# Norms of q and k with tokens on partitions in a convolution-attention kernel

## The chip, the cores and the metric

The kernel runs on one core of one Trainium2 chip. The time is the device time of one execution in microseconds (us); the time of a kernel is the median of several runs. A core has five engines that work side by side and meet through semaphores: PE (TensorE, matrix products from SBUF into PSUM), DVE (VectorE), ACT (ScalarE), POOL (GpSimd) and SP (which here only starts transfers). Each runs its own instructions in order. POOL and SP start the transfers (DMA). PEld is the loading of the stationary operand of a product; it is listed apart from PE.

## What is computed

The network has two layers: a convolution attention on a 64 x 64 image of 256 channels, then a bidirectional state-space block and a mixture of experts on the 4096 tokens. The change touches the first layer alone:

```python
qkv = concat([conv(x, W1, 0), conv(x, W3, 1), conv(x, W5, 2)], axis=1)
qkv = conv(qkv, Wdw, 1, groups=3 * c)          # 3x3, each channel by itself
q, k, v = split(qkv, 3, axis=1)                # 8 heads of 32 channels
n = sqrt(sum(t * t, axis=-1, keepdims=True))   # over the 32 channels of a head
t = t / maximum(n, 1e-12)                      # for t = q and t = k
attn = softmax(einsum('bhnc,bhmc->bhnm', q, k) * temperature)
```

So each token needs, for q and for k, eight norms, one per head, and each of its 256 values is divided by the norm of its head. q is also multiplied by the temperature of its head.

## The kernel before

All values are fp32. `conv_phase` (from L174) keeps channels on partitions: 256 channels are two halves t = 0, 1 of 128 partitions, so a half holds four heads. Tokens run along the free dimension, in eight chunks of N = 512.

**Order.** Everything from L605 on stands in a manual schedule: each engine runs its instructions in the order in which the program issues them. The work is cut into twelve units (kind, half of the image, t): four units of k, then q and v in turn, four of each. A unit of k or v makes 6 or 8 products by Winograd's method (L452, 6 or 10 matrix products of 512 columns in each), a unit of q makes 4 plain ones (L444). `feed` issues products ahead, up to three results (four PSUM buffers, pool `a_pcv`). `transform_out` combines the results on DVE (`out_t`, `pad`; ACT copies every second result out of PSUM first, tile `c`, L481), in groups of two. `depthwise` of a unit runs during the unit after it: ACT starts it with the first tap of two pieces (L524), DVE adds the other eight taps of each (L528, 16 instructions). In each group of a unit the program issues, in this order: the combination, `feed`, `tick`, the steps of `depthwise`, and "fills" (transforms of the weights, `wx` and `wo`, and of the inputs, `v`).

**Norms.** When `depthwise` of a unit of q or k has ended, its finished rows wait in `rows_left` as chunks of 128 channels x 512 tokens: three for the upper part of the image, five for the lower. `norm_sums` takes up to three chunks at a time, and the next three only once these are done. It has three steps, each one `tick` after the one before it:

- `norm_sums`: ACT squares each chunk (`sq`, L550) and PE multiplies the squares by `heads` (L551). `heads` is the stationary operand, 128 x 32, and the 512 columns of `sq` move. Each chunk's result has 32 partitions of its own in one PSUM tile (`ps`, tag ps0): eight copies of each head's sum.
- `norm_inverse`: over up to 96 partitions x 512 tokens, DVE takes the maximum with 1e-24 (L558), ACT the square root (L559), DVE the reciprocal (L560). PE spreads the four rows of each chunk over its 128 channels by a product with `pick`, or `pick_q`, which holds the temperature (L565; 32 partitions, 512 columns).
- `norm_apply`: DVE multiplies the chunk by the result in PSUM (L275, `acc<-acc,ps`). For q, ACT puts the columns into another order (`qo`, L574). POOL starts the store (L578).

The program has twelve such rounds, here called g1 to g12. The column "DVE next" is the first instruction on DVE behind L560.

| round | chunks | squares on PE (L551) | maximum (L558) | spread on PE (L565) | DVE next |
|---|---|---|---|---|---|
| g1 | 3 | 151.72 | 166.93 | 171.80 | 171.57 |
| g2 | 3 | 225.23 | 239.73 | 244.60 | 244.37 |
| g3 | 3 | 301.82 | 312.82 | 337.39 | 317.47 |
| g4 | 3 | 355.82 | 356.99 | 374.18 | 361.64 |
| g5 | 3 | 385.74 | 386.90 | 391.78 | 391.56 |
| g6 | 3 | 420.51 | 427.69 | 442.60 | 432.33 |
| g7 | 1 | 461.03 | 472.71 | 477.48 | 477.35 |
| g8 | 3 | 497.79 | 504.20 | 527.46 | 508.85 |
| g9 | 2 | 549.63 | 550.75 | 567.97 | 555.40 |
| g10 | 3 | 582.96 | 584.13 | 611.62 | 591.51 |
| g11 | 3 | 666.64 | 694.13 | 703.14 | 705.25 |
| g12 | 2 | 709.41 | 711.87 | 716.75 | 718.82 |

(us from the start of the span, in the profile of before.) `heads`, `pick` and `pick_q` are made on DVE and PE at the very start (L227 to L260), among the statistics of the input (L611), outside the manual schedule.

**Buffers.** `sq`, `c`, `wx`, `wo`, `qo` and the copies of v share one pool of six buffers (`a_t`, tag "t"). `heads`, `pick` and `pick_q` lie in the pool `a_one` with the large tiles; `rn` lies in `a_r`. The pools close at the end of `conv_phase`. Then `Early` loads weights of the second layer (`win`, `wx`, `wdt`, L746 to L752) and `attention_phase` loads `wpj`, q and k (L832 to L850), all on SP's queue, in this order.

Of the kernel before, what the change touches and what calls it, by code (L numbers as in the profile page):

```python
# [14 lines left out]
FP = mybir.dt.float32  # L15
# [3 lines left out]
AF = mybir.ActivationFunctionType  # L19
ALU = mybir.AluOpType  # L20
AX = mybir.AxisListType
# [3 lines left out]
P = 128  # L25
# [3 lines left out]
CT = C // P  # L29
N = 512  # L30
# [143 lines left out]
def conv_phase(cx, xT, w1, w3, w5, temp, qd, kd, vd, uk, uv):  # L174
# [13 lines left out]
    nc, tc = cx.nc, cx.tc  # L188
# [3 lines left out]
    with ExitStack() as ctx:  # L192
        one = ctx.enter_context(tc.tile_pool(name="a_one", bufs=1))
        up = ctx.enter_context(tc.tile_pool(name="a_u", bufs=3))
        rp = ctx.enter_context(tc.tile_pool(name="a_r", bufs=1))
        tp = ctx.enter_context(tc.tile_pool(name="a_t", bufs=6))
        accp = ctx.enter_context(tc.tile_pool(name="a_acc", bufs=3))
        pcv = ctx.enter_context(tc.tile_pool(name="a_pcv", bufs=4, space=PSUM))
        pms = ctx.enter_context(tc.tile_pool(name="a_pms", bufs=1, space=PSUM))
# [24 lines left out]
        for t in range(CT):  # L224
            nc.sync.dma_start(out=wq[:, t, :], in_=w1[t, 0, :, 0, :])

        heads = one.tile([P, 32], FP, name="heads")  # L227
        pick = one.tile([P, P], FP, name="pick")
        nc.vector.tensor_reduce(
            pick.rearrange("p (a b) -> p a b", b=32)[:, :, 0:1], cx.ident.rearrange("p (a b) -> p a b", b=32),  # L230
            AX.X, ALU.add,
        )
        nc.vector.tensor_copy(
            heads.rearrange("p (a b) -> p a b", b=8),
            pick.rearrange("p (a b) -> p a b", b=32)[:, :, 0:1].to_broadcast([P, 4, 8]),
        )
        first_of = one.tile([P, 32], FP, name="first_of")
        nc.vector.memset(first_of, 0.0)
        for h in range(4):
            nc.vector.memset(first_of[:, 8 * h : 8 * h + 1], 1.0)  # L240
        rep = one.tile([P, 4], FP, name="rep")
        for h in range(4):
            nc.vector.tensor_reduce(
                rep[:, h : h + 1], cx.ident.rearrange("p (j a) -> p a j", a=32)[:, 8 * h, :], AX.X, ALU.add
            )
        nc.vector.tensor_copy(pick.rearrange("p (a b) -> p a b", b=32), rep[:, :, None].to_broadcast([P, 4, 32]))

        pick_q = []
        for t in range(CT):
            x = tp.tile([P, 4, 32], FP, name="px", tag="t")  # L250
            nc.vector.tensor_scalar(
                x, heads[:, None, :].to_broadcast([P, 4, 32]), temp[:, t : t + 1], None, ALU.mult
            )
            y = one.tile([P, 4, 32], FP, name=f"px{t}")
            nc.vector.tensor_tensor(y, x, first_of[:, None, :].to_broadcast([P, 4, 32]), ALU.mult)
            ps = pms.tile([P, N], FP, name="ps", tag=f"ps{t}")
            nc.tensor.transpose(ps[:, 0:P], y.rearrange("p a b -> p (a b)"), cx.ident)
            pq = one.tile([P, P], FP, name=f"pick_q{t}")
            nc.vector.tensor_copy(pq, ps[:, 0:P])
            pick_q.append(pq)  # L260

        wdw = one.tile([P, 54], FP, name="wdw_s")
        for kind, f in ((0, 1.0), (1, -1.0 / 6.0), (2, -2.0 / 9.0)):
# [10 lines left out]
        def plus(out, x, y, op=ALU.add):  # L274
            nc.vector.tensor_tensor(out, x, y, op)  # L275
# [231 lines left out]
        def depthwise(kind, half, t, pad):  # L507

            row0, n = (LAG, H - LAG) if half else (0, LAG)
            ch = {"q": 0, "k": CT, "v": 2 * CT}[kind] + t  # L510
            dst = accp.tile([P, (H - LAG) * W], FP, name="acc", tag="acc")

            def piece(b, tap):
                dy, dx = divmod(tap, 3)
                m = n // 2
                return (
                    dst[:, m * W * b : m * W * (b + 1)].rearrange("p (h w) -> p h w", w=W),
                    pad[:, m * b + dy : m * b + dy + m, dx : dx + 4, :].rearrange("p h s j -> p h (s j)"),
                    wdw[:, 9 * ch + tap : 9 * ch + tap + 1],
                )  # L520

            for b in range(2):
                o, src, w_ap = piece(b, 0)
                nc.scalar.activation(o, src, AF.Copy, scale=w_ap)  # L524
            for b in range(2):
                for tap in range(1, 9):
                    o, src, w_ap = piece(b, tap)
                    nc.vector.scalar_tensor_tensor(o, src, w_ap, o, ALU.mult, ALU.add)  # L528
                    yield
                if kind == "v":  # L530
                    turn(dst, t, row0 * W // P, n * W // P // 2 * b, n * W // P // 2)
            if kind != "v":
                c0 = row0 // ROWS
                rows_left.extend((dst[:, N * j : N * j + N], kind, t, c0 + j) for j in range(n // ROWS))
                if not busy:
                    norm_sums()
# [3 lines left out]
        def norm_sums():  # L540

            chunks = rows_left[:3]
            del rows_left[:3]
            busy[:] = chunks
            if not chunks:
                return
            ps = pms.tile([P, N], FP, name="ps", tag="ps0")
            for j, (a, _, _, _) in enumerate(chunks):
                sq = tp.tile([P, N], FP, name="sq", tag="t")
                nc.scalar.activation(sq, a, AF.Square)  # L550
                nc.tensor.matmul(ps[32 * j : 32 * j + 32, :], heads, sq, start=True, stop=True)  # L551
            later(lambda: norm_inverse(chunks, ps))

        def norm_inverse(chunks, ps):

            n = 32 * len(chunks)
            rn = rp.tile([P, N], FP, name="rn", tag="rn")
            nc.vector.tensor_scalar(rn[0:n, :], ps[0:n, :], 1e-24, None, ALU.max)  # L558
            nc.scalar.activation(rn[0:n, :], rn[0:n, :], AF.Sqrt)  # L559
            nc.vector.reciprocal(rn[0:n, :], rn[0:n, :])  # L560
            back = []
            for j, (_, kind, t, _) in enumerate(chunks):
                back.append(pms.tile([P, N], FP, name="ps", tag=f"ps{j}"))
                r = slice(32 * j, 32 * j + 32)
                nc.tensor.matmul(back[j], (pick_q[t] if kind == "q" else pick)[r, :], rn[r, :], start=True, stop=True)  # L565
            later(lambda: norm_apply(chunks, back))

        def norm_apply(chunks, back):
            for (a, kind, t, c), ps in zip(chunks, back):
                plus(a, a, ps, ALU.mult)  # L570
                if kind == "q":

                    s = tp.tile([P, N], FP, name="qo", tag="t")
                    nc.scalar.copy(  # L574
                        s.rearrange("p (h j r) -> p h r j", j=TX, r=4), a.rearrange("p (h r j) -> p h r j", r=4, j=TX)
                    )
                    a = s
                nc.gpsimd.dma_start(out=(qd if kind == "q" else kd)[t][:, N * c : N * c + N], in_=a)  # L578
            norm_sums()

# [13 lines left out]
        def later(f, lag=1):  # L594
            events.append((clock[0] + lag, f))
# [9 lines left out]
        with tc.manual_schedule(engines=ORDERED):  # L605
# [13 lines left out]
            ps = pms.tile([P, N], FP, name="ps", tag="ps0")  # L619
# [7 lines left out]
            ps = pms.tile([P, N], FP, name="ps", tag="ps1")  # L627
# [1337 lines left out]
def kernel(  # L1965
# [45 lines left out]
    nc.vector.tensor_scalar(beyond, hottest, SAFE, None, ALU.is_gt)  # L2011

    conv_phase(cx, xT, w1, w3, w5, temp, qd, kd, vd, uk, uv)
    with tc.tile_pool(name="early", bufs=1) as pool:
        early = Early(cx, pool, w_in, w_x, w_dt)
# [105 lines left out]
```

## Time and profile before

| what | us |
|---|---|
| three runs | 4383.31, 4386.24, 4386.42; median 4386.24 |
| the profiled execution | 4368.56 |
| its span, first to last instruction | 4366.8 |
| busy over the span: PE, DVE, ACT, POOL | 3693.8, 3600.9, 2685.7, 1563.3 |
| first product of the attention (L953) | starts at 730.18 |
| squares on ACT, L550, 128x512 | 32 of 0.621 |
| squares times heads on PE, L551 | 64 records, 18.9 busy |
| maximum, L558, 96x512 | 9 of 0.681 (64x512: 2; 32x512: 1) |
| square root, L559, 96x512 | 9 of 0.629 |
| reciprocal, L560, 96x512 | 9 of 3.349 (64x512: 3.345; 32x512: 3.341) |
| spread on PE, L565 | 64 records, 19.5 busy |
| multiplication, L275 `acc<-acc,ps` | 32 of 0.681 |
| reordering of q, L574 | 16 of 1.125 |
| first tap on ACT, L524 | 0.922 (768 columns), 1.346 (1280 columns) |

One fp32 product shows as two records on PE and two on PEld. In the timeline each entry merges neighbours of one kind: its start, the time from the first start to the last end, engine, line, operation, out<-in, shapes, the number of instructions, and in brackets how long the engine had been idle and what ended that. The convolution phase fills about the first 722 us of the span; the attention and all that follows are not edited.

### The profile page before, as it was taken

To read this page: it belongs to the slowest core of one execution; us is meant where nothing else is said; L and a number is where in the kernel's file an instruction comes from. 1 tells how busy PE (TensorE), PEld (TensorE's weight loads), DVE (VectorE), ACT (ScalarE), POOL (GpSimd) and SP (SyncE) were. 2 spreads that over 40 slices of the span, in tenths; PEclk is the share of its full clock that TensorE was granted. 3 is DMA by queue.
4 is the path that set the end of the run, shared out by engine and by line. 5 is a ranking of instruction groups with operands and counts; after the bars stand their busy time and mean duration, and the time that the engine had idled before them with its cause. 6 is when DMAs were issued, how large, how long until landed. Compare 5 with 4: busy or idle time off the path is not lost. (4 is left out here: it accounts for less than half of the span.)

```text
span 4366.8 us, 43278 instructions
## 1 busy us (share of the span) xinstructions
PE 3693.8 (85%) x15072; PEld 1180.6 (27%) x15072; DVE 3600.9 (82%) x2976; ACT 2685.7 (62%) x4175; POOL 1563.3 (36%) x1051
## 2 busy tenths in 40 slices
PE   4659895999999999997878788888788788876698
PEld 2224341222222222222222222222222222221243
DVE  6887876888879879778899999999999999999311
ACT  1012223888788888776677777777777777774122
POOL 2210000000000000002677677776767777776000
PEclk9879996999999999998888989989888898977799
DMA  4322223000000000003332334443323334332121
GB/s 148 125 77 93 75 79 129 4 30 11 25 23 18 16 23 18 11 23 118 104 108 98 103 124 119 123 119 107 127 82 124 124 114 118 120 109 84 63 63 37
DMA packets 150243, 351.18 MB, mean 80 GB/s; under 512 B 35461, under 2 KB 44421, under 8 KB 149502
## 3 DMA queue, kind: packets, MB, share of 16 engines
q1 hardware_dynamic: 139214, 313.17, 23.1%
q0 software_dynamic: 10800, 35.14, 2.3%
q8 instruction: 120, 1.97, 0.2%
q14 instruction: 109, 0.89, 0.1%
HBM read 268.69 MB, written 79.56 MB: 80 GB/s over the span
## 5 line engine op out<-in xcount | busy, mean ns | idle before, releaser
L1669 POOL TENSOR_TENSOR dbx<-dtxr,b 128x1024 f32<-128x1024 f32 x512 | 1205.8, 2360 | 467.7 <-DVE da L1677 320.7
L1677 DVE TENSOR_TENSOR_SCAN da<-da,state,dbx 128x1024 f32<-128x1024 f32 x512 | 1203.2, 2350 | 62.0 <-ACT state L1700 33.6
L960 ACT ACTIVATE e<-sc 128x1024 f32<-128x1024 f32 x1024 | 992.8, 1023 | 204.7 <-PE sc L953 161.2
L881 DVE TENSOR_TENSOR s<-s,e 128x1024 f32<-128x1024 f32 x768 | 880.6, 1216 | 44.7 <-ACT e L960 44.2
L1659 ACT ACTIVATE da<-dtr,aneg 128x512 f32<-128x512 f32 x1024 | 708.3, 692 | 36.0 <-DMA dtr<-dtd 3.8
L953 PE MATMUL sc<-q,kS 32*128 32x512 f32 x4096 | 653.6, 644 | 20.4 <-DMA kS<-kd 11.4
L1682 DVE TENSOR_TENSOR h<-da,c 128x1024 f32<-128x1024 f32 x512 | 627.2, 1225 | 37.7
L888 PE MATMUL av<-e,vT 128*32 128x512 f32 x4096 | 549.8, 608 | 3.7 <-ACT o L894 3.7
L1709 PE MATMUL y<-h,sel 128*32 128x512 f32 x2048 | 442.0, 675 | 130.9 <-DVE h L1682 130.7
L132 POOL TENSOR_TENSOR ln_few<-ln_few,minus_half 128x4 f32<-128x4 f32 x29 | 29.4, 1015 | 1417.8 <-DMA ln_few<-ln_row 1417.8
L452 PE MATMUL cv<-v,u 128*128 128x512 f32 x928 | 422.2, 615 | 64.4 <-DVE pad L272 27.4
L953 PEld LDWEIGHTS sc<-q,kS 32*128 32x128 f32 x4096 | 211.3, 183 | 466.9 <-issue 244.4
L1250 PE MATMUL mm<-u,win 128*128 128x512 f32 x496 | 267.2, 688 | 72.0 <-DMA u<-ud 52.4
L1700 ACT COPY state<-da 128x2 f32<-128x2 f32 x511 | 80.5, 158 | 362.5 <-DVE h L1682 360.0
L452 PEld LDWEIGHTS cv<-v,u 128*128 128x128 f32 x928 | 182.1, 198 | 302.9 <-issue 230.9
L528 DVE SCALAR_TENSOR_TENSOR acc<-pad,wdw_s,acc 128x768 f32<-128x768 f32 (+1 forms) x192 | 244.5, 1279 | 19.4 <-ACT acc L524 13.3
L1294 PE MATMUL mm<-xp,taps 128*128 128x512 f32 x480 | 221.3, 609 | 6.0 <-DVE m L1441 5.1
L881 DVE TENSOR_TENSOR s<-e 128x1024 f32<-128x1024 f32 x128 | 150.8, 1219 | 71.6 <-ACT e L960 71.4
L888 PEld LDWEIGHTS av<-e,vT 128*32 128x32 f32 x4096 | 81.3, 108 | 396.6 <-issue 379.0
L1709 PEld LDWEIGHTS y<-h,sel 128*32 128x32 f32 x2048 | 60.4, 114 | 468.5 <-DVE h L1682 292.8
L1250 PEld LDWEIGHTS mm<-u,win 128*128 128x128 f32 x496 | 104.2, 221 | 244.8 <-issue 127.0
L504 ACT COPY pad<-pad 128x480 f32<-128x480 f32 x12 | 7.1, 594 | 214.2 <-DVE pad L272 214.1
(338 smaller groups left out, 3747.3 us busy)
## 6 DMA issues: line engine op xcount, KB each, us to landing
dtr<-dtd SPq DMA_DIRECT2D x128, 512.0 KB
dtxr<-dtd SPq DMA_DIRECT2D x128, 512.0 KB
b<-bcd SPq DMA_DIRECT2D x64, 256.0 KB
c<-bcd SPq DMA_DIRECT2D x64, 256.0 KB
dtd<-dt SPq DMA_DIRECT2D x64, 256.0 KB
dtd<-few SPq DMA_DIRECT2D x64, 256.0 KB
u<-uv SPq DMA_DIRECT2D x24, 640.0 KB
u<-ud SPq DMA_DIRECT2D x16, 512.0 KB
```

The source lines that it names most:

```text
L452: nc.tensor.matmul(rows4(ps), u[:, dy, P * ci : P * ci + P], v[:, dy : dy + HR, ci, :], start=dy + ci == 0, stop=dy == k - 1 and ci == CT - 1,
L528: nc.vector.scalar_tensor_tensor(o, src, w_ap, o, ALU.mult, ALU.add)
L881: nc.vector.tensor_tensor(z, x, y, ALU.add)
L888: nc.tensor.matmul(g.av[32 * h : 32 * h + 32, :], vT[:, kb, P * t + 32 * h : P * t + 32 * h + 32], es[h // 2][:, h % 2, :], start=kb == 0, ...
L953: nc.tensor.matmul(ps[h // 2][:, h % 2, :], kS[r, t, P * kb : P * kb + P], q_t[r, t, :], start=True, stop=True,)
L960: nc.scalar.activation(e, ps[i], AF.Exp)
L1250: nc.tensor.matmul(ps, win[d][:, t, P * e : P * e + P], u[:, t, ::-1] if d else u[:, t, :], start=t == 0, stop=t == CT - 1,)
L1659: nc.scalar.activation(da[:, v, :], dts[i, e, j][0][:, v, :], AF.Exp, scale=aneg[i % 2][:, a : a + 1])
L1669: nc.gpsimd.tensor_tensor(u, dts[i, e, j][1], bcs[i, k][0][:, None, :].to_broadcast([P, 2, N]), ALU.mult)
L1677: nc.vector.tensor_tensor_scan(da, da, u, state[i % 2][:, 4 * e + j, k : k + 1], ALU.mult, ALU.add)
L1682: nc.vector.tensor_tensor(h, da, bcs[i, k][1][:, None, :].to_broadcast([P, 2, N]), ALU.mult)
L1709: nc.tensor.matmul(ys[i, e][32 * j : 32 * j + 32, :], cx.sel, hs[n + j // 2][:, j % 2, :], start=False, stop=k == SQ - 1,)
```

## The change

The squares become the stationary operand and `heads`, now 128 x 4, the moving one, so a sum over channels comes out with 128 tokens on partitions and 4 heads in columns; a chunk has four such products, and three chunks fill 48 columns of one PSUM tile. Maximum, square root and reciprocal then work on 128 x 48. ACT copies the 16 columns of each chunk 32 times each (tile `x`, 128 x 512, pool `a_t`), and PE brings them back to channels on partitions by four products with the identity, with `x` stationary. `pick`, `pick_q` and what makes them are gone; the temperature of q is now multiplied in by `norm_apply`.

```diff
-        heads = one.tile([P, 32], FP, name="heads")
-        pick = one.tile([P, P], FP, name="pick")
...
-            pick_q.append(pq)
+        heads = one.tile([P, 4], FP, name="heads")
+        nc.vector.tensor_reduce(heads, cx.ident.rearrange("p (a b) -> p a b", b=32), AX.X, ALU.add)
...
                 nc.scalar.activation(sq, a, AF.Square)
-                nc.tensor.matmul(ps[32 * j : 32 * j + 32, :], heads, sq, start=True, stop=True)
+                for i in range(N // P):
+                    nc.tensor.matmul(
+                        ps[:, 16 * j + 4 * i : 16 * j + 4 * i + 4], sq[:, P * i : P * i + P], heads,
+                        start=True, stop=True,
+                    )
             later(lambda: norm_inverse(chunks, ps))
...
-            n = 32 * len(chunks)
-            rn = rp.tile([P, N], FP, name="rn", tag="rn")
-            nc.vector.tensor_scalar(rn[0:n, :], ps[0:n, :], 1e-24, None, ALU.max)
-            nc.scalar.activation(rn[0:n, :], rn[0:n, :], AF.Sqrt)
-            nc.vector.reciprocal(rn[0:n, :], rn[0:n, :])
+            n = 16 * len(chunks)
+            rn = rp.tile([P, 48], FP, name="rn", tag="rn")
+            nc.vector.tensor_scalar(rn[:, 0:n], ps[:, 0:n], 1e-24, None, ALU.max)
+            nc.scalar.activation(rn[:, 0:n], rn[:, 0:n], AF.Sqrt)
+            nc.vector.reciprocal(rn[:, 0:n], rn[:, 0:n])
             back = []
-            for j, (_, kind, t, _) in enumerate(chunks):
+            for j in range(len(chunks)):
+                x = tp.tile([P, 16, 32], FP, name="rx", tag="t")
+                nc.scalar.copy(x, rn[:, 16 * j : 16 * j + 16, None].to_broadcast([P, 16, 32]))
+                x = x.rearrange("p (i h) c -> p i (h c)", h=4)
                 back.append(pms.tile([P, N], FP, name="ps", tag=f"ps{j}"))
-                r = slice(32 * j, 32 * j + 32)
-                nc.tensor.matmul(back[j], (pick_q[t] if kind == "q" else pick)[r, :], rn[r, :], start=True, stop=True)
+                for i in range(N // P):
+                    nc.tensor.matmul(back[j][:, P * i : P * i + P], x[:, i, :], cx.ident, start=True, stop=True)
...
             for (a, kind, t, c), ps in zip(chunks, back):
-                plus(a, a, ps, ALU.mult)
                 if kind == "q":
+                    nc.vector.scalar_tensor_tensor(a, ps, temp[:, t : t + 1], a, ALU.mult, ALU.mult)
...
+                else:
+                    plus(a, a, ps, ALU.mult)
```

More of the change, by code (lines that the diff above doesn't have):

```diff
@@ L225, in conv_phase @@
             nc.sync.dma_start(out=wq[:, t, :], in_=w1[t, 0, :, 0, :])
-        heads = one.tile([P, 32], FP, name="heads")
-        pick = one.tile([P, P], FP, name="pick")
[L229 to L259, printed above, removed]
-            pick_q.append(pq)
+        heads = one.tile([P, 4], FP, name="heads")
+        nc.vector.tensor_reduce(heads, cx.ident.rearrange("p (a b) -> p a b", b=32), AX.X, ALU.add)
         wdw = one.tile([P, 54], FP, name="wdw_s")
```

## The prediction

> **What bounds the kernel now.** The chain of waits on the page covers only the last 4 us of the span, so I read the convolution phase engine by engine. First DVE's waits between 100 and 725 us: whom it waited for, the total, how often, the longest.
>
> ```profile
> DVE out_t L275 <- ACT c L481: 27.0, 5, 10.8
> ...
> DVE rn L560 <- ACT rn L559: 15.3, 12, 4.9
> DVE acc L275 <- PE ps L565: 14.8, 5, 5.0
> DVE rn L558 <- PE ps L551: 13.9, 4, 4.7
> ```
>
> DVE waits for PE's products in places only (ACT's copy `c` waits for PE itself). The timelines of both engines, laid side by side, show where, and give six stages. **A**, to about 30 us: DVE, with the input's statistics. **B**, 105 to 306: DVE has hardly a wait but for weights whose load it releases itself; PE idles. **C**, 306 to 426: PE runs without a gap but 1.35 us at 391.78; DVE waits for it. **D**, 426 to 494: DVE is solid, PE waits at the end (11.2 us). **E**, 494 to 664: PE again, but for short waits around the transposes of v. **F**, 664 to 730: nothing overlaps; taps, g11, g12 and the first loads of the attention follow one another. So a us saved on DVE counts in B and D, a us added on PE in C and E. Next, DVE's and ACT's timelines at g2:
>
> ```profile
> 239.73 0.68 DVE L558 TENSOR_SCALAR rn<-ps 96x512 f32<-96x512 f32 x1
> 241.10 3.35 DVE L560 RECIPROCAL rn<-rn 96x512 f32<-96x512 f32 x1 [0.70 <-ACT rn L559]
> 244.37 9.39 DVE L528 SCALAR_TENSOR_TENSOR acc<-pad,wdw_s,acc 128x1280 f32<-128x1280 f32 x6
> ```
> ```profile
> 240.44 0.63 ACT L559 ACTIVATE rn<-rn 96x512 f32<-96x512 f32 x1 [10.98 <-DVE rn L558]
> 240.98 2.60 ACT L524 ACTIVATE acc<-pad,wdw_s 128x1280 f32<-128x1280 f32 x2
> ```
>
> The round holds DVE from 239.73 to 244.37, 4.64 us. Note the second ACT line: right behind the root ACT makes the first taps, which DVE needs as soon as the reciprocal is done; today they are ready long before. Then PE's steps, and the two forms nearest to the new ones: 16 records with a 128x128 stationary operand and one column moving, and four with 128 columns.
>
> ```profile
> 337.39 1.13 PE L565 MATMUL ps<-rn,pick 32*128 32x512 f32 x6
> 338.46 1.98 PE L452 MATMUL cv<-v,u 128*128 128x512 f32 x4
> ...
> 355.82 1.06 PE L551 MATMUL ps<-sq,heads 128*32 128x512 f32 x6
> 356.81 3.70 PE L452 MATMUL cv<-v,u 128*128 128x512 f32 x8
> ```
> ```profile
> 421.50 0.66 PE L587 MATMUL tr<-ident,acc 128*128 128x128 f32 x4
> ...
> 4053.97 1.95 PE L158 MATMUL tl<-mean_mat,hn 128*128 128x1 f32 x16 [2.40 <-ACT hn L153]
> ```
>
> Start to next start, a spread takes 1.07 us and a squares step 0.99 for three chunks at once (two chunks: 1.06 and 0.98, g9). Last, SP's own waits, and the start of the attention:
>
> ```profile
> SPq L746 <- PE ps L565: 80.0, 1, 80.0
> ```
> ```profile
> 716.75 2.08 PE L565 MATMUL ps<-rn,pick_q 32*128 32x512 f32 x4 [4.91 <-DVE rn L560]
> ...
> 730.18 3.78 PE L953 MATMUL sc<-q,kS 32*128 32x512 f32 x12 [11.36 <-DMA kS<-kd]
> ```
>
> SP's first load for the next phase waits for the last product that reads `pick_q`, though PE read the convolution's large tiles for the last time at about 664; I read this as the pool `a_one` being handed over as a whole. From that load's start (718.98) to the first score product are 11.2 us.
>
> **The change, part by part.** *PE's price.* L158: the last of 16 records starts 1.70 us after the first, 0.11 each, with the granted clock at 1.00; the same form at 4090.18 takes 0.21 at 0.53. A new spread record moves 128 columns: L452 takes 0.43 for 512, so 0.107, and the four transposes of 421.50 (0.27 each, 0.66 together) show loads and 128 columns overlapping at 0.13 or less. I take 0.11 for both steps: three chunks have 24 records, 2.64 us; two have 16, 1.76. Bound from above for the spread: load and product one after the other, 0.217. So at full clock squares cost +1.65, a spread +1.57; with two chunks +0.78 and +0.70.
>
> *DVE's and ACT's price.* Maximum 128x48 from PSUM: 0.21, between 0.166 (the logits, 128x8 from PSUM, L1832) and 0.68. Root: 0.26, as 128x4 (0.263) and 128x64 (0.248). Reciprocal: 0.44, on the line through 128x16 (0.244, L924) and 512 columns (3.349). Three hand-overs of 0.03. The round's path to the end of the reciprocal is 1.00. The copies `rx`: 0.49 apart, as three `pad` copies of 512 columns (1.54 in all); bound from above 1.12, the strided `qo`. The multiplication keeps its 0.68 (L272 of this shape from PSUM: 0.683).
>
> *A wait takes the place of the reciprocal.* In program order the three `rx` come between the root and the first taps. ACT now waits for the reciprocal, copies three times (1.47) and only then makes the first tap (0.92 or 1.35), for which DVE stands. DVE goes on at 1.00 + 1.47 + 0.92 + 0.04 = 3.43, or 3.86, instead of 4.64: g1 gains 1.2 us rather than 3.6, g2 and g6 0.8. Behind DVE's wait stand the other taps and the weights; nobody else is late. g7 has one chunk and no tap behind it: 4.64 - 0.73 = 3.9.
>
> *A.* Removing L233 to L259 frees DVE from 10.97 to 12.05, 12.65 to 13.04 and 13.69 to 13.89: 1.67. The input still arrives at 377 to 401 GB/s until 18.2; behind it in the queue are 320 KB, 0.8 us. So the last part lands at about 17.4, its statistics now start at 18.68: gain 1.3 (0 to 1.67).
>
> *B.* -1.2 - 0.8 = -2.0. *C.* g3 spread +1.57, g4 squares +1.65, g4 spread +1.57, g5 +1.87 (squares 2.64, eight records of q 3.7, spread 2.64, against 7.11 with the wait for the reciprocal, which is gone), g6 squares +1.65: +8.3. *D.* -0.8 - 3.9 = -4.7. *E.* g8 squares: ten records at the clock of an idle PE (0.21) and 14 at 0.11, 3.64 against 2.01: +1.6; spread +1.57; g9 +0.78 + 0.70; g10 +1.65 + 1.57, less the 1.08 for which the transposes at 616.86 wait for DVE: +6.8.
>
> *F.* The root of g11 starts at 699.08, held by ACT's copies of v, as now. Then 0.75 to the reciprocal's end (699.8), `rx` (700.4), three chunks of eight records at 0.21 (granted clock here 0.50): 705.8. Multiplication 706.5, `qo` 707.6, squares 708.2, two chunks on PE to 711.9. There `heads` is read for the last time, nothing of `a_one` is used after it, and SP's loads go out at 712.0 instead of 718.98: -6.9. The rest of g12 then runs beside them: reciprocal 712.9, spread to 717.3, `qo` to 719.2, before the first scores at 723.2. If SP went on waiting for the last spread, the gain were 1.5.
>
> [...]
>
> *Nothing.* The six buffers of `a_t` now also hold `rx` until a spread that can be 20 us late (g3: 317 to 337). There the third `sq` waits for it, and the first taps behind it until about 340; DVE needs them at 345.58. That slack is the cover; without it DVE would lose at most 9 us. The twelve rounds issue no DMA but those of before.
>
> **Sum**: -1.3 - 2.0 + 8.3 - 4.7 + 6.8 - 6.9 = +0.2 us. Against the profiled execution (4368.56, its span and 1.8 around it) that is 4368.8; the median of the runs shown lies 17.7 above that execution, and I carry the difference over: **4386.4**. All phases behind 730 shift as a whole.
>
> **The rivals.** *1. The spread's loads do not hide.* If load and product of a spread record follow each other, each costs 0.107 more. On the path are the spreads of g3, g4, g5, g8, g10 (24 records) and g9 (16): 136, +14.6: **4401**, slower. For it: a load alone shows 0.19 on PEld, more than the 0.107 of its product. Against: the transposes. It decides the sign from 0.063 us a record (8.6 / 136).
>
> *2. PE's added work is taken in by waits in C and E.* Then +15.1 falls away: **4371**, faster. For it: PE waits for ACT's copies of v around each set of transposes, and PE runs up to three products ahead. Against: between 307 and 421 PE shows one gap, and each `c` that DVE waits for ends a row of products without one.
>
> *3. SP's loads keep the last spread as their release*: +5.4, **4392**; still no change that can be told.
>
> *4. The reciprocal does not shrink*, if its time were per instruction. Then g7 and F lose what they gain: 4386.4 + 3 x 2.9 and 2 x 2.9 in B: about **4401**. Against it: 0.244 for 128x16.
>
> **How the numbers follow.** 0.2% of the time, 8.8 us, is about what a measurement of this kernel tells from no change. No change (with rival 3): 0.55, around 4386, its own range 4379 to 4393. Rivals 1 and 4 and smaller sorts of dearer PE work: 0.25. Rival 2, and DVE's waits for the first taps smaller than I make them (up to 8 us in g1, g2 and g6 together): 0.20. The range reaches to near rivals 2 and 1: 4373 to 4401.
>
> **What would show it.** Right: 24 records of L551 and of the spread in about 2.6 us each at full clock; L560 at about 0.44; a wait of DVE's first taps (L528) for L524 of some 2.4 us at g1; the first score at about 730 with L746 seven us before the end of the last spread's round. Wrong: records of the spread 0.2 apart at full clock (rival 1); c at g6 not later by 5 us or so against g3 (rival 2); L746 behind the last spread (rival 3). What would make the whole wrong is a stage whose engine I mistook, above all D, if PE's lateness at 426 leaves DVE waiting there.

## The result, and the profile after

| | before | changed |
|---|---|---|
| median of 20 runs each, same chip | 4384.22 (4373.5 to 4391.93) | 4388.98 (4382.99 to 4398.29) |
| ratio, 95% interval | 1 | 1.0016 [1.0008, 1.0023] |
| profiled execution | 4368.56 | 4386.82 |
| its span | 4366.8 | 4384.9 |
| first score product starts | 730.18 | 733.50 |

The changed kernel is slower by about 7 us by the ratio (0.16%; the interval excludes 1 and reaches 1.0023); the two medians are 4.8 us apart. In the two profiles 3.3 us of it have arisen by the first score product; the other 14.8 us of the difference of the spans lie behind it, in code that nobody edited. The loop of the state-space block alone, from its first `dbx` on POOL to its last, takes 1985.7 us in the profile of before, 2000.8 in that of the changed kernel and 1988.0 to 1998.4 in the eleven other profiles of this study. I take that for scatter: the loop is the same code in all of them, and the profile of before happens to be the shortest and that of the changed kernel the longest. So single profiles are compared here only up to the first score product.

DVE's waits between 100 and 725 us (total, times, longest): first a row of the kernel before, then the changed kernel.

```profile
DVE acc L528 <- ACT acc L524: 13.3, 4, 4.2
```
```profile
DVE out_t L243 <- ACT c L449: 43.7, 7, 13.5
DVE acc L496 <- ACT acc L492: 31.1, 10, 5.2
DVE rn L530 <- PE ps L520: 20.9, 5, 6.1
...
DVE rn L532 <- ACT rn L531: 11.8, 11, 5.0
```

The reciprocal is cheap now, but DVE's sum of waits for PE (through the copy `c`) rose from 27.0 to 43.7, that for the first taps from 13.3 to 31.1. DVE and then ACT at g2, changed kernel:

```profile
239.50 0.19 DVE L530 TENSOR_SCALAR rn<-ps 128x48 f32<-128x48 f32 x1
240.00 0.45 DVE L532 RECIPROCAL rn<-rn 128x48 f32<-128x48 f32 x1 [0.31 <-ACT rn L531]
243.44 9.49 DVE L496 SCALAR_TENSOR_TENSOR acc<-pad,wdw_s,acc 128x1280 f32<-128x1280 f32 x6 [2.99 <-ACT acc L492]
```
```profile
239.73 0.24 ACT L531 ACTIVATE rn<-rn 128x48 f32<-128x48 f32 x1 [10.45 <-DVE rn L530]
240.49 1.65 ACT L536 COPY rx<-rn 128x512 f32<-128x512 f32 x3 [0.52 <-DVE rn L532]
242.05 2.61 ACT L492 ACTIVATE acc<-pad,wdw_s 128x1280 f32<-128x1280 f32 x2
```

The round still holds DVE for 3.94 us (239.50 to 243.44), 2.99 of it a wait for the tap that ACT makes behind the three copies. PE in stage C:

```profile
355.76 2.74 PE L520 MATMUL ps<-heads,sq 128*128 128x4 f32 x24
358.35 17.41 PE L420 MATMUL cv<-v,u 128*128 128x512 f32 x40
375.60 2.84 PE L540 MATMUL ps<-ident,rx 128*128 128x128 f32 x24
...
388.58 2.74 PE L520 MATMUL ps<-heads,sq 128*128 128x4 f32 x24
391.18 5.38 PE L412 MATMUL cv<-xpad,wq 128*128 128x512 f32 x8
396.39 2.84 PE L540 MATMUL ps<-ident,rx 128*128 128x128 f32 x24
```

Start to next start, squares take 2.59 us and a spread 2.68 instead of 0.99 and 1.06. And one thing is new: the eight records of q behind the squares of g5 take 5.38 us; in the kernel before they took 3.70:

```profile
386.73 3.70 PE L444 MATMUL cv<-xpad,wq 128*128 128x512 f32 x8
```

Then SP and PE at the end of the phase:

```profile
722.75 0.33 SPq L723 DMA_DIRECT2D win<-in_w_in  x1
```
```profile
719.24 3.36 PE L520 MATMUL ps<-heads,sq 128*128 128x4 f32 x16 [2.45 <-ACT sq L518]
724.34 3.79 PE L540 MATMUL ps<-ident,rx 128*128 128x128 f32 x16 [1.74 <-ACT rx L536]
733.50 3.79 PE L930 MATMUL sc<-q,kS 32*128 32x512 f32 x12 [5.38 <-DMA kS<-kd]
```

The first load goes out right behind the squares of g12 and ahead of their spread. Measured by stage from these two profiles (A: maximum of g1; B: DVE's hold at g1 and g2; C: from the maximum of g3 to the first `out_t` of g6, 426.49 and 435.31; D: to PE's start at 494.07 and 498.12; E: to the last `pad`, 664.24 and 675.55; F: to the first score):

| stage | forecast | measured |
|---|---|---|
| A | -1.3 | +0.8 |
| B | -2.0 | -1.8 (g1 4.64 to 3.51, g2 4.64 to 3.94) |
| C | +8.3 | +9.7 |
| D | -4.7 | -4.8 |
| E | +6.8 | +7.3 |
| F | -6.9 | -8.0 |
| sum | +0.2 | +3.3 (the rows make 3.2; 0.1 lies between A and C) |

### The profile page after: what moved, and what is told of

Read it like the earlier page. It is cut to its first block, busy times and chain, and to the rows that moved or that the text cites. A ratio compares the mean times of both kernels' runs of the same rounds, so it can differ in the third digit from the quotient of the medians.

```text
span 4384.9 us, 44082 instructions
## 1 busy us (share of the span) xinstructions
PE 3729.0 (85%) x15454; PEld 1247.8 (28%) x15454; DVE 3562.4 (81%) x2959; ACT 2701.1 (62%) x4207; POOL 1563.5 (36%) x1051
## 5 line engine op out<-in xcount | busy, mean ns | idle before, releaser
L496 DVE SCALAR_TENSOR_TENSOR acc<-pad,wdw_s,acc 128x768 f32<-128x768 f32 (+1 forms) x192 | 245.1, 1282 | 36.8 <-ACT acc L492 31.1
```

## The experiments

Eleven kernels were run. The table has their anchors from one profile each, us from the start of the span, and the ratio to the kernel before on the same chip. The changed kernel, profiled twice, gave 733.50 and 734.48, so a difference of about 1 us between two anchors says nothing.

| run | max g3 | max g6 | max g7 | max g11 | first score | ratio [95%] |
|---|---|---|---|---|---|---|
| before | 312.82 | 427.69 | 472.71 | 694.13 | 730.18 | 1 |
| changed | 311.93 | 436.51 | 481.05 | 705.44 | 733.50 | 1.0016 [1.0008, 1.0023] |
| e11 changed again | 312.33 | 436.93 | 481.47 | 706.54 | 734.48 | 1.0014 [1.0005, 1.0024] |
| e1 own pool, old | 312.63 | 427.57 | 472.59 | 694.05 | 720.12 | 0.9966 [0.9953, 0.9980] |
| e2 own pool, new | 311.70 | 436.29 | 480.84 | 705.24 | 729.34 | 0.9994 [0.9984, 1.0004] |
| e3 taps first | 307.30 | 435.25 | 477.62 | 704.08 | 732.11 | 0.9992 [0.9981, 1.0002] |
| e4 spread twice | 313.96 | 448.65 | 493.20 | 729.57 | 759.43 | 1.0045 [1.0031, 1.0058] |
| e5 plus narrow | 313.63 | 441.29 | 486.31 | 726.61 | 765.66 | 1.0099 [1.0081, 1.0117] |
| e6 plus wide | 315.90 | 443.80 | 488.81 | 725.26 | 764.99 | 1.0077 [1.0060, 1.0094] |
| e7 e2 and e3 | 306.77 | 434.42 | 476.77 | 703.20 | 727.38 | 0.9994 [0.9985, 1.0003] |
| e8 mixed | 307.89 | 421.72 | 466.73 | 684.85 | 708.50 | 0.9946 [0.9929, 0.9962] |
| e9 wide squares | 312.07 | 431.63 | 476.31 | 700.67 | 728.86 | 0.9986 [0.9976, 0.9997] |
| e10 e9, taps first | 307.57 | 427.22 | 469.71 | 693.65 | 721.65 | 0.9972 [0.9961, 0.9983] |

**What releases the loads (e1, e2).** In the kernel before:

```diff
+        own = ctx.enter_context(tc.tile_pool(name="a_own", bufs=1))
...
-        heads = one.tile([P, 32], FP, name="heads")
-        pick = one.tile([P, P], FP, name="pick")
+        heads = own.tile([P, 32], FP, name="heads")
+        pick = own.tile([P, P], FP, name="pick")
...
-            pq = one.tile([P, P], FP, name=f"pick_q{t}")
+            pq = own.tile([P, P], FP, name=f"pick_q{t}")
```

> The kernel before, with heads, pick and the two pick_q in a small pool of their own; nothing else is changed. My theory: the first loads of the attention (win and those behind it) wait for the last reader of anything in the pool a_one; without these four tiles the last reader is DVE's last tap, so win goes out at about 694 to 700 us instead of 719, its data are in before PE is through with the last spread (718.8), and the first score product starts at 719 to 721 instead of 730.2. Time: 9 to 11 us below before, ratio about 0.9977. Rival: the loads wait for something else at the end of the phase (the stores of q, the acc buffers); then win stays at 719, the first score at 730, ratio 1.000.

SP and PE of that run:

```profile
694.23 0.33 SPq L747 DMA_DIRECT2D win<-in_w_in  x1
```
```profile
SPq L747 <- DVE acc L529: 30.0, 1, 30.0
```
```profile
716.66 2.07 PE L566 MATMUL ps<-rn,pick_q 32*128 32x512 f32 x4 [4.91 <-DVE rn L561]
720.12 3.78 PE L954 MATMUL sc<-q,kS 32*128 32x512 f32 x12 [1.39 <-issue]
```

The load now waits for DVE's last tap (L529), starts 24.8 us earlier, and the score product follows the last spread with no wait for a transfer: 10.1 us gained without touching the norms. The same edit in the changed kernel (`heads` alone goes into `own`):

> The changed kernel, with heads in a small pool of its own. My theory: win goes out behind DVE's last tap, at about 705.5 instead of 722.8, and the first score then waits for PE alone, which ends the last spread at 728.1: first score at about 728.3 instead of 733.5, 5 us below the changed kernel, so about 2 us above before (ratio 1.0004 where the changed kernel has 1.0016). If the pool has nothing to do with it: win at 722.8 and 1.0016.

`win` went out at 705.42 and the first score started at 729.34, 4.2 us earlier. Both show what the forecast only read from the queue: the pool `a_one` was handed over as a whole, and its last reader released the loads. Most of the changed kernel's gain in F is this release: from the maximum of g11 to the first score the changed kernel is 8.0 us shorter than before (28.06 and 36.05), and with the pool apart in both only 2.0 (24.10 in e2, 26.07 in e1). It can be had by moving four tiles. (The gains in the ratios are larger, 0.34% and 0.22%; with the scatter behind 730 us I don't put a cause to the rest.)

**Where ACT's order costs (e3).** In the changed kernel the copies and the spread become a function of their own that waits for the next step of `depthwise`:

```diff
             nc.vector.reciprocal(rn[:, 0:n], rn[:, 0:n])
+            behind.append(lambda: norm_spread(chunks, rn))
+
+        def norm_spread(chunks, rn):
...
                         step(before)
+                        while behind:
+                            behind.pop(0)()
```

> The changed kernel with ACT's rx copies and the spread issued one step later, behind the first taps, so that ACT makes the first taps right after the root. My theory (the gain of the short reciprocal in B and D is lost to ACT's order): DVE's stop at g1, g2 and g6 shrinks from 3.5, 3.9 and 3.9 us to 1.4 to 1.9, no wait for L492 over 1.5 us is left there; together 6 to 8 us below the changed kernel, about at the time of before (ratio 0.9998 to 1.0003). Rival: DVE in B waits for the weights in any case, and what it saves at g1 and g2 comes back as a wait for PE; then the stops are as short but the end of B (the last v input before stage C) does not move, and the time is 1.0016 times before, as the changed kernel's.

DVE at g2 in that run:

```profile
237.36 0.45 DVE L532 RECIPROCAL rn<-rn 128x48 f32<-128x48 f32 x1 [0.31 <-ACT rn L531]
238.61 9.49 DVE L496 SCALAR_TENSOR_TENSOR acc<-pad,wdw_s,acc 128x1280 f32<-128x1280 f32 x6 [0.80 <-ACT acc L492]
```

The stop shrank as expected, 3.94 to 1.76 us, and the maximum of g3 came 4.6 us earlier. But my theory fell on the total: at the maximum of g6 only 1.3 us were left, and 1.4 at the first score. (The ratio, 0.9992, would fit the theory, but what it has beyond the 1.4 us arose behind 730 us.) Up to the first score the rival was nearer, though not by its mechanism: PE did start stage C 4.4 us earlier (the products of v at 305.77 against 310.16). PE behind the squares of g4:

```profile
352.49 2.74 PE L520 MATMUL ps<-heads,sq 128*128 128x4 f32 x24
355.08 19.11 PE L420 MATMUL cv<-v,u 128*128 128x512 f32 x40
```

The same 40 records took 17.41 us in the changed kernel. In this run's windows (length, then busy time of PE, PEld, DVE, ACT and POOL with instructions, granted clock, DMA share, GB/s):

```profile
350.00:355.00 5.00, 5.00 (x31) 3.56 (x29) 0.00 (x0) 0.00 (x0) 0.00 (x0) 1.00 0.26 51
355.00:360.00 5.00, 5.00 (x10) 2.20 (x11) 4.30 (x6) 1.90 (x4) 0.00 (x0) 0.66 0.21 83
```

The clock is granted at 0.66, behind a squares step, with PE busy all the time.

**The map of stages (e4).**

```diff
-                for i in range(N // P):
+                for i in list(range(N // P)) * 2:
                     nc.tensor.matmul(back[j][:, P * i : P * i + P], x[:, i, :], cx.ident, start=True, stop=True)
```

> The changed kernel with each spread product issued twice (the second writes the same values); nothing is left out. It prices a record and tests the map of stages. My theory: 136 records more on the path in C and E, at 0.11 us each: +15; in F 24 at 0.21 for g11: +5, and nothing for g12, whose spread lies beside the first loads; none in B and D. Together +20 us over the changed kernel, ratio to before 1.006. Rival (PE's added work is taken in by waits in C and E): only the +5 of F, ratio 1.0028. Rival (load and product do not overlap, 0.2 a record at full clock): +30, ratio 1.0085. A three-chunk spread should show 48 records in 5.3 us at clock 1.00.

PE of that run:

```profile
361.10 2.74 PE L520 MATMUL ps<-heads,sq 128*128 128x4 f32 x24
363.70 19.11 PE L420 MATMUL cv<-v,u 128*128 128x512 f32 x40
382.64 5.52 PE L540 MATMUL ps<-ident,rx 128*128 128x128 f32 x48
```

48 records in 5.52 us are 0.115 each, not 0.217: load and product overlap, so rival 1 of the prediction is out. Stage D is free of charge, as mapped (maximum of g6 to that of g7: 44.55 us against 44.54). C and E together lengthen by 22.1 us (705.44 to 729.57, less the 2.0 at g3), not by nothing, so rival 2 is out too; nor by the 15 forecast. F (from the maximum of g11 on) took 1.8 instead of 5, and 2.0 were lost by the maximum of g3, where nothing was expected (0.6 of it already at the maximum of g1, the rest while DVE waited longer for the weights `wr`). Part of the excess stands in the second line: 40 records at 19.11 instead of 17.41, again behind the squares. The ratio, 1.0045, lies between theory (1.006) and rival (1.0028), and its interval holds neither: it says 20 us over before where the first score is 29 us late. I go by the anchors.

**A first test of the clock, which missed (e5, e6).** The kernel before, with four more products for each chunk of a squares step; with `heads[:, 0:4]` moving in e5 and the identity in e6.

```diff
                 nc.tensor.matmul(ps[32 * j : 32 * j + 32, :], heads, sq, start=True, stop=True)
+                more = pms.tile([P, N], FP, name="ps", tag="ps1")
+                for i in range(N // P):
+                    nc.tensor.matmul(more[:, P * i : P * i + P], sq[:, P * i : P * i + P], cx.ident, start=True, stop=True)
```

> The kernel before with four products more for each chunk of a squares step, in the changed kernel's form (the squares stationary, four columns moving) into a PSUM tile that nobody reads; the normalization itself stays the old one. Theory: such products count as little work for the granted clock, so that after 24 of them in 2.6 us the clock falls for some 5 us (0.5 to 0.7) behind some of the squares steps of C and E (g5, g6, g8), and this is what made g5 and g6 dearer than forecast. Then this kernel is 2 to 8 us slower than the one with wide products. PE's own work on the path: C and E 5 x 2.6 + 1.75 = 14.8, F 3.4: 18 us over before, ratio 1.0042, with the clock 1.0047 to 1.006. Rival: the clock falls for reasons of its own, as it does in the kernel before; then no more falls than with wide products, and 1.0042.

> As the run with narrow products added, but with 128 columns of the identity moving in place of four: the same loads, the same number of records, 0.107 us of columns each. Theory: granted clock 1.00 behind the squares steps of C and E wherever the kernel before has it, +18 us over before, ratio 1.0042 or somewhat less. Rival: the same falls as with narrow products, and the same time.

Both cost far more than forecast, 43 and 33 us, and up to the first score they differ by 0.7 us, so they don't tell the theories apart. PE at g4 in e6:

```profile
357.82 1.04 PE L551 MATMUL ps<-sq,heads 128*32 128x512 f32 x2
358.80 1.16 PE L554 MATMUL ps<-ident,sq 128*128 128x128 f32 x8
359.88 1.05 PE L551 MATMUL ps<-sq,heads 128*32 128x512 f32 x2
```

One old squares product takes 0.98 us by itself, as long as three in a row took before: the step grew by 5.1 us, not by 2.6. And the wide old products between them kept 24 narrow records from standing in a row.

**The clock, tested on the changed kernel (e9, e10, e11).** The squares products move 128 columns in place of four; loads and records stay as many.

```diff
+        heads_w = one.tile([P, 32, 4], FP, name="heads_w")
+        nc.vector.tensor_copy(heads_w, heads[:, None, :].to_broadcast([P, 32, 4]))
...
+                ps.append(pms.tile([P, N], FP, name="ps", tag=f"ps{j}"))
                 for i in range(N // P):
                     nc.tensor.matmul(
-                        ps[:, 16 * j + 4 * i : 16 * j + 4 * i + 4], sq[:, P * i : P * i + P], heads,
-                        start=True, stop=True,
+                        ps[j][:, P * i : P * i + P], sq[:, P * i : P * i + P],
+                        heads_w.rearrange("p a b -> p (a b)"), start=True, stop=True,
```

> The changed kernel, whose squares products move 128 columns (heads repeated 32 times) in place of four, into one PSUM bank for each chunk; the maximum then takes three instructions. Same records, same loads. Theory (four moving columns count as little work, and the granted clock falls behind 24 of them in a row): the clock stays at 1.00 from 390 to 400 and from 426 to 440 us, eight records of q products take 3.7 us instead of 5.4 at g5, the first c after the squares of g6 comes 4 us earlier against g4; stage E likewise behind g8; less about 1 us for the maxima (three for one: 0.35 each in B, D and F). First score product at 728 to 730 instead of 733.5. Rival (the clock falls whenever it does, or for the loads): the same rows of 0.67 and 0.50 and first score at 733 to 735.

PE at g5 in e9:

```profile
386.39 2.84 PE L523 MATMUL ps<-heads_w,sq 128*128 128x128 f32 x24
389.07 3.60 PE L414 MATMUL cv<-xpad,wq 128*128 128x512 f32 x8
392.51 2.84 PE L547 MATMUL ps<-ident,rx 128*128 128x128 f32 x24
```

and the window behind the squares of g5, first in the changed kernel, then in e9:

```profile
390.00:395.00 5.00, 5.00 (x18) 2.70 (x19) 1.50 (x3) 2.83 (x6) 0.00 (x0) 0.68 0.01 5
```
```profile
390.00:395.00 5.00, 5.00 (x30) 3.55 (x29) 2.24 (x4) 4.71 (x8) 0.42 (x1) 1.00 0.02 3
```

The squares step is 0.1 us longer (2.68), and what follows runs at the full clock: 3.44 us start to next start for the eight q records, where the changed kernel needed 5.21. Stage C (maximum of g3 to that of g6) falls from 124.58 to 119.56 us. Behind g6 the clock still dips, among the transposes (0.90 and 0.76 in 425 to 435; the changed kernel has 0.50 and 0.54 in 430 to 440), and E gains nothing in sum (224.36 against 224.39): 1.9 us are won between the maxima of g8 and g9 and lost again later. Ratio 0.9986 against 1.0014 on the same chip.

> The last edit together with the first taps ahead of the rx copies. The first taps alone moved the end of B 4.6 us forward, and 3.4 of these were gone by the maximum of g6. Theory (they were lost to half clocks behind the squares steps, of g4 above all): with 128 moving columns the maximum of g6 and the first score stay 4 us ahead of the run with wide squares alone, first score at 722 to 726. Rival (stage C starts when PE does, and PE's start is bound by something else than DVE): again only 1 to 1.5 us ahead.

Here the lead of 4.5 us at the maximum of g3 is still 4.4 at g6, 6.6 at g7 and 7.2 at the first score. What e3 lost, it lost to the clock: of 3.4 us between these maxima, 1.1 went in the first 60 records of v (26.87 us for 25.75, the clock at 0.70 from 305 to 310) and 1.7 in the 40 behind the squares of g4.

This run also settles what e9 leaves open. In these profiles half clock comes in stretches of 3.41 us or whole multiples (changed kernel: 391.83 to 395.25, and 429.38 to 439.62), with edges 3.41 us apart, and what followed a step went with where it lay between these edges. In the changed kernel the squares of g5 (388.58 to 391.18) lie whole in one stretch, 388.42 to 391.83, and the next is at half clock; those of g4 lie across the edge at 357.70, and no half clock follows. In e9 the squares of g5 lie across an edge too, at 388.02, so that step alone could owe its full clock to its place. The squares of g4 in e10 do not:

```profile
349.07 2.84 PE L523 MATMUL ps<-heads_w,sq 128*128 128x128 f32 x24
```
```profile
350.00:355.00 5.00, 5.00 (x26) 3.27 (x25) 2.96 (x7) 1.90 (x4) 0.00 (x0) 1.00 0.45 134
355.00:360.00 5.00, 5.00 (x13) 2.18 (x12) 2.84 (x3) 0.00 (x0) 0.00 (x0) 1.00 0.00 0
```

They lie whole in the stretch from 349.05 to 352.46, as the narrow ones of g4 in e3 do in 352.38 to 355.79; e3 has half clock in the next stretch, e10 the full one. So the rival (the clock falls whenever it does, or for the loads) is out for C.

> The changed kernel itself, beside the two with wide squares on the same chip. First score at 733.5 within 0.3 (runs with the same first 690 us agreed so far to 0.3), and the ratio near 1.0008 to 1.0016: 3.3 us are what the first 730 us show, anything over that lies behind.

734.48, 1.0 us later and so outside the 0.3, with the ratio as forecast.

**Both together (e7), and each form where it pays (e8).** e7 is e2 and e3 in one.

> The changed kernel with heads in a pool of its own and the first taps ahead of the rx copies, both edits together. If they are independent: 5 + 7 = 12 us below the changed kernel, 5 us below before: ratio about 0.999. If the rounds at the end of the phase are delayed by the later spread, less of the 5: 1.000.

727.38: 6.1 us, about the sum of what the two gave alone (4.2 and 1.4) and not of what I had expected of them. e8 has both edits and keeps the old form in the rounds where PE sets the pace:

```diff
+            rounds[0] += 1
+            narrow = rounds[0] in (1, 2, 7, 11, 12)
...
+                if not narrow:
+                    nc.tensor.matmul(ps[32 * j : 32 * j + 32, :], heads, sq, start=True, stop=True)
+                    continue
...
+            later(lambda: (norm_inverse if narrow else old_inverse)(chunks, ps))
```

> Both forms in one kernel: the new form for the rounds on which DVE or the serial end counts (g1, g2, g7, g11, g12), the old one for those on which PE counts (g3 to g6, g8 to g10); heads, heads4, pick and pick_q in a pool of their own; the first taps ahead of the rx copies. My map of stages says: A 0, B -6, C 0, D -3.9, E 0, F -13 (loads hidden, short reciprocals): 23 us below before, ratio 0.9948. First score product at 707 to 709 instead of 730.2. If the map is wrong and PE's work in C and E does not count: no better than the changed kernel with both edits (ratio 0.998 or more).

SP and PE at the end of the phase in e8:

```profile
685.03 0.33 SPq L798 DMA_DIRECT2D win<-in_w_in  x1
```
```profile
703.83 3.78 PE L584 MATMUL ps<-ident,rx 128*128 128x128 f32 x16 [1.69 <-ACT rx L580]
708.50 3.78 PE L1005 MATMUL sc<-q,kS 32*128 32x512 f32 x12 [0.89 <-issue]
```

21.7 us ahead of before at the first score, about 24 us by the ratio (the medians are 4356.42 and 4381.30 us): the fastest kernel of the study. It is 6.0 us ahead of before at the maximum of g6 and 9.3 at that of g11; the end of the phase (maximum of g11 to the first score) takes 23.65 us instead of 36.05. And the 4.9 us won by g3 last through C and E, where no narrow squares stand.

## Why the prediction was right, and where it was not

No change was forecast as the likeliest, 4386.4 us in 4373 to 4401; the median is 4388.98. The sum of the terms was 3.1 us too low. That the total came so near is in part luck. The median carried over, 4386.24, was 2.0 us above that of the 20 later runs of the same kernel, and the misses in A (2.1) and C (1.4) were partly made up by F (1.1).

- **DVE and the hand-overs: right.** Maximum 0.19 (0.21), root 0.24 (0.26), reciprocal 0.45 (0.44), copies 1.65 (1.54). The wait for the first tap at g1 was 2.56 us (some 2.4), and B and D came out within 0.2 us. e3 shows the reason too: with the taps first the stop at g2 falls to 1.76 us.
- **PE's price of a step: right.** 2.59 and 2.68 us against 2.64. Rivals 1 and 4 needed 0.2 a record and a reciprocal as long as before; neither is there. e4 ends rival 2.
- **F: right in kind, 1.1 us better.** The last read of `heads` releases the loads, as argued from the queue; rival 3 is out. The load went out 47.2 us after the stage's start (722.75 less 675.55); 712.0 less 664.24 is 47.8.
- **C: the mechanism was right, a size was off, and a cause was missing.** "g5 +1.87 (squares 2.64, eight records of q 3.7, spread 2.64 ...)" took the q products at their old duration. Squares, q products and spread took 2.60, 5.21 and 2.68, and with four more records of q behind them 12.21 us in place of 8.93: +3.28. The transposes behind g6 took 4.98 in place of 3.84, another 1.1. The other four steps of the sum (squares of g4 and g6, spreads of g3 and g4) cost the +6.4 forecast, and the rest of the stage was 1.1 shorter than before, so the miss is 1.4. Both excesses are a granted clock of 0.5 to 0.7 behind the squares; e9 brings the full clock back behind g5, and e10 behind a step that lies whole in one stretch. The working charged a record only for its own time, not for what it does to the clock of those behind it.
- **E: right in sum, by an exchange.** The squares of g8 took 2.63 us and not 3.64, since the full clock was back at 501.06; the four records of q behind them took 3.11 in place of 1.82, at half clock again from 504.47 to 507.89.
- **A: wrong.** "So the last part lands at about 17.4, its statistics now start at 18.68: gain 1.3 (0 to 1.67)." The statistics ended only 0.5 us earlier (19.48 for 19.98, the start of L612's second instruction, L589 in the changed kernel): DVE waited 4.4 us for the input instead of 3.5. By 92.6 that was gone too, where PE waits for the weights `u` in both kernels (it goes on at 92.60 before, at 92.65 in the changed kernel). Then PE had half clock until 98.29 instead of 96.63, and DVE's combination that waits for it came at 106.64 instead of 105.79: this is the +0.8 at the maximum of g1. In e3 and e7, which have the same start, the half clock ended at 96.38 and 95.49, and the maximum came at 166.72 and 166.84 against 166.93 before: no gain, and a scatter of the size of the term.
- **The median carried over: open.** Taking all behind 730 us as shifted as a whole holds only within the scatter of the loop told of above. 3.3 us of the 7 in the ratio are seen; the rest isn't placed. In the experiments, too, the ratio and the first score differ by up to 10 us, either way (e4: 20 and 29 us behind before; e5: 43 and 35).

## What to carry to other kernels

Swapping the operands of these small products moved work from DVE (for three chunks 3.4 us less in maximum and reciprocal) to PE (3.2 more in squares and spread at full clock) and ACT (1.3 more in root and copies), so ask round by round which engine sets the pace there: here the new form, with ACT's taps first, was worth about 12 us in five rounds (720.12 less 708.50) and the fix of a pool 10, while in the other seven rounds the new form cost 17 (C and E). A price for a new step on PE needs the granted clock behind it too (at g5 the same eight records of q took 5.21 us behind narrow squares and 3.44 behind wide ones). And a transfer that waits for the last reader of a whole pool can go out earlier when a few small tiles with late readers are moved to a pool of their own (24.8 us earlier in e1).

## What the runs showed of the hardware

- **Behind most rows of narrow products the clock fell, though PE had no gap.** 24 records with four columns moving, in 2.6 us, were followed by a granted clock of 0.66 to 0.68 over 5 us at g5 in the changed kernel and at g4 in e3 (PE busy for 5.00 of these 5.00 us), but by 1.00 at g4 in the changed kernel; with 128 columns moving (e9, e10), by 1.00 in all of C but the transposes behind g6. The rows agree with half clock by stretches of 3.41 us. Five profiles with narrow squares (changed, e3, e4, e7, e11) have 25 steps of 24 records in C and E, and behind 19 of them the next stretch is at half clock. In the changed kernel and e11 these are six steps that lie whole in one stretch (2.6 us); the other four cover at most 2.01 us of one, and the next is at full clock. Of the ten such steps with 128 columns moving (e9, e10) five cover 2.36 to 2.68 us of one stretch, and the next is at full clock behind all ten. Records and loads are as many in both forms, and PE was busy for 5.00 of 5.00 us at g4 in both e3 and e10; so in these steps the clock went with what the records moved, and not with PE being occupied.
- **Three products with 32 stationary columns each ran in the time of one.** 0.98 us alone in e6, 0.99 for three in a row in the kernel before, each into 32 partitions of its own. With other products between them, in e6, each took its 0.98: 2 us more a step.
